# Edge scores of a graph attention layer with the leaky relu split, one decoding of the edge counts, and shorter lags between gathers, exponentials and scatters

## The chip, the cores and the metric

The kernel runs on one core of a Trainium2 chip, in one launch. The metric is device time in microseconds (us); the figure of the kernel before is the median of five runs. A profile is one further execution, recorded by the hardware profiler, and has a time of its own. Engines are named as the profile names them: PE is the matrix engine (PEld its weight loads), DVE the vector engine, ACT the scalar engine, POOL the GpSimd engine, SP the engine that issues most of the plain DMAs.

## The reference

A two-layer graph network on 625 nodes with 1024 features and 10,000 edges, sorted by their destination. Each layer adds to x the output of a graph layer and of a linear attention, both on the normalised x, and then that of a feed-forward block. Layer 0 has the graph attention that the change is about; layer 1 has two mean-aggregating layers, a linear attention, and a full attention with a mixture of experts. The graph attention, cut to what matters (h is 4 heads, d is 64):

```python
xl = (x @ Wl).reshape(n, H, D)          # 625 x 4 x 64
xr = (x @ Wr).reshape(n, H, D)
msg = xl[src] + xr[dst]                 # one row for each edge, and for each node with itself
act = jnp.where(msg > 0, msg, 0.2 * msg)
e = jnp.einsum('ehd,hd->eh', act, att)
p = jnp.exp(e - segment_max(e, dst)[dst])
alpha = p / (segment_sum(p, dst)[dst] + 1e-16)
out = segment_sum(alpha[..., None] * xl[src], dst)
```

An edge between the same two nodes may occur several times.

## The kernel before

Nodes lie in five tiles of 125 rows (t = 0 to 4). The whole computation is the function `attempt`, which is called with `shifted=False`; it leaves out the maximum in the softmax. Tests on the size of what occurred are collected in the columns of `inside`; if one fails, a second `attempt(shifted=True)` runs after the first (`again`), and computes the safe form.

Since a softmax weight depends only on the pair (source, destination), the kernel makes two dense tables. `CT` counts how often each pair occurs, and `table` in DRAM holds exp(score) for each pair. Then `weigh` (product in L743) multiplies a tile of the table, read back by `load_table` as `tb`, with the counts, which gives `pT`, and PE sums `pT` against xl1 (`pg`). xl1 holds the xl rows of each node, 64 for each head, and a 65th column for the denominator.

The counts are made on PE. For each of 79 columns of 128 edges (`EN`), DVE writes two one-hot rows into `ring` (L414, L416; up to 8 columns ahead), and PE adds five products to the PSUM tile `pct` (L437). To hold two destinations in one number, a count of the upper half of the destinations is weighted with 4096. `decode` (L448 to L456) takes the two apart on DVE. It runs three times, after columns 27, 53 and 79 (`counting`), and after each the counting pauses for two steps (`held`).

The scores are made on DVE for 40 groups, each of two columns of edges (the last has one column of 16 edges). The group's rows are gathered by POOL with four indirect DMAs, two into `ga` from xl and two into `gb` from xr (L578; four buffers of each kind). `score_group` adds them (L586) and calls `score` (L555): leaky relu (L557), product with `att` (L558), sum over each head's 64 (L559), and a clip at 60 (L561). ACT takes the exponential (L565), and POOL writes the group's results to `table` with two indirect DMAs (L592). The same for a node with itself is done by `self_loops` (L601), five times, on rows that lie in SBUF; there L607 also copies the xl rows into xl1.

The order on each engine is the order in which the program emits the work. `do` delays a stream's parts, so that preparation, PE work and what follows it are interleaved. `work(us)` (L613) is a clock by estimate: callers report PE time, and after each 7.6 us one beat g is emitted, in this order: a self loop (g = 1 to 5), the exponential of group g-4, the score of group g-3, then in turn the gathers of group g and the scatters of group g-5. So with 40 groups there are 45 beats. POOL and DVE work through these in order; each waits where its data or a buffer is not ready. The 79 column counts lie among the keys and values of the linear attention (two halves of five tiles, with up to six counts after each tile), and after them come its queries and answers (m = 0 to 7; `oT`), with the first products of the output projection (`mixed`, L668, `px`). Beats that are then left are emitted at once (L691), then `load_table(0)`, the sums of the weights of the feed-forward block (`weight_sums`, L707), their mean on PE (`pm`), the rest of `mixed`, and `weigh(0)`.

Later, in layer 1, the degrees of the nodes come out of another count (`pdeg`), with a test on the largest one (L1031, L1032), and the tests in `inside` are summed by a product on PE (`prt`).

Of the kernel before, what the change touches and what calls it, by code (L numbers as in the profile page):

```python
# [8 lines left out]
FP = mybir.dt.float32  # L9
# [4 lines left out]
AF = mybir.ActivationFunctionType  # L14
ALU = mybir.AluOpType
# [18 lines left out]
NB_MIN = 10  # L34
FAR = -1.0e30
LIMIT = 60.0
LEAST, MOST = 1.0e-22, 1.0e25
MAGIC = 12582912.0
BIG = 1.5 * 2.0**35

# [12 lines left out]
def attempt(ctx: ExitStack, tc: tile.TileContext, w: dict, out: bass.AP, shifted: bool):  # L53
# [26 lines left out]
    nc.vector.memset(blockmask[0:64, 0:64], 1.0)  # L80
    nc.vector.memset(blockmask[64:128, 64:128], 1.0)

    inside = const.tile([128, 3], FP, name="inside")
    nc.vector.memset(inside, 1.0)

    def test(col, src, n, pool):
# [251 lines left out]
    with ExitStack() as st0:  # L338
# [8 lines left out]
        with ExitStack() as edges:  # L347
# [51 lines left out]

            pad(xnT)  # L400
            nc.vector.memset(xl1[:, :, :, 64:65], 1.0)

            counting = [(lo, hi, t) for lo, hi in ((0, 27), (27, 53), (53, EN)) for t in range(lo, hi)]
            part = dict(done=0, held=0)
            made_ahead = []

# [10 lines left out]
            def count():  # L419

                if part["held"] or part["done"] == EN:
                    return False
                lo, hi, t = counting[part["done"]]
                part["held"] = 2 * (t == hi - 1)

                def prep():
                    while len(made_ahead) < min(8, EN - t):
                        one_hot()
                    hold["hot"] = made_ahead.pop(0)
                    part["done"] += 1  # L430

                def pe():
                    od, os = hold["hot"]
                    if t == lo:
                        part["pc"] = psums[-1][0].tile([128, NT, 512], FP, tag="pct", name="pct", bufs=1)
                    for j in range(NT):
                        nc.tensor.matmul(part["pc"][:P, j, :HN], lhsT=os[:, nodes(j)],  # L437
                                         rhs=od[:, :HN], start=(t == lo), stop=(t == hi - 1))

                def decode():  # L440
                    for j in range(0, NT, 2):
                        js = slice(j, min(j + 2, NT))
                        n = js.stop - j
                        low, high, v = CT[:, js, 0:HN], CT[:, js, HN:NP], part["pc"][:P, js, :HN]
                        low_r, high_r = CTr[:, js, 0:HN], CTr[:, js, HN:NP]
                        u = pool.tile([P, 2, HN], FP, tag="u", name="u", bufs=1)[:, 0:n, :]

                        nc.vector.tensor_scalar(u, v, 1728.0, BIG, op0=ALU.subtract, op1=ALU.add)  # L448
                        nc.vector.tensor_scalar(u, u, BIG, None, op0=ALU.subtract)
                        if lo == 0:  # L450
# [12 lines left out]
                do(prep, pe, decode if t == hi - 1 else None)  # L463
                return True
# [87 lines left out]

            def score(dst, m, n, p):  # L555

                nc.vector.scalar_tensor_tensor(m, m, 0.2, m, op0=ALU.mult, op1=ALU.max)  # L557
                nc.vector.tensor_tensor(m, m, att[0:p].unsqueeze(1).to_broadcast([p, n, 256]), op=ALU.mult)  # L558
                nc.vector.tensor_reduce(dst, m.rearrange("p t (h e) -> p t h e", h=4), AX.X, ALU.add)  # L559
                if not shifted:  # L560
                    nc.vector.tensor_scalar(dst, dst, LIMIT, None, op0=ALU.min)  # L561
# [20 lines left out]
            def score_group(g):  # L582
                lo, n, p = groups[g]
                a, b = ab.pop(g)
                m = a[0:p, 0:n, :]
                nc.vector.tensor_tensor(m, m, b[0:p, 0:n, :], op=ALU.add)  # L586
                score(es[0:p, lo:lo + n, :], m, n, p)

            def scatter(g, j):
                lo, n, p = groups[g]  # L590
                if j < n:
                    nc.gpsimd.indirect_dma_start(  # L592
                        out=table[:, :],
                        out_offset=bass.IndirectOffsetOnAxis(ap=at[0:p, lo + j:lo + j + 1], axis=0),
                        in_=es[0:p, lo + j, :], in_offset=None)

            own = pool.tile([P, NT, 4], FP, name="own")

            diagonal = table[0:N * (N + 1), :].rearrange("(s d) h -> s d h", d=N + 1)[:, 0, :]

            def self_loops(t):  # L601

                m = pool.tile([P, 1, 256], FP, tag="xd", name="gs", bufs=1)
                nc.vector.tensor_tensor(m[:, 0, :], xlr[:, t, 0:256], xlr[:, t, 256:512], op=ALU.add)
                score(own[:, t:t + 1, :], m, 1, P)
                exp(own[:, t:t + 1, :])
                nc.vector.tensor_copy(xl1[:, t, :, 0:64], xlr[:, t, 0:256].rearrange("p (h e) -> p h e", h=4))  # L607
                rows_dma(nc.scalar, diagonal[nodes(t), :], own[:, t, :])


# [1 line left out]

            def work(us):  # L613
                beat["us"] += us
                while beat["us"] >= 7.6 * beat["g"] and beat["g"] < len(groups) + 5:
                    g = beat["g"]
                    beat["g"] += 1
                    if 1 <= g <= NT:
                        self_loops(g - 1)
                    if 4 <= g < len(groups) + 4:  # L620
                        lo, n, p = groups[g - 4]
                        exp(es[0:p, lo:lo + n, :])
                    if 3 <= g < len(groups) + 3:
                        score_group(g - 3)
                    for j in range(G):
                        if g < len(groups):
                            gather(g, j)
                        if g >= 5:
                            scatter(g - 5, j)

            work(0.0)
            states = []
# [55 lines left out]
            nc.sync.dma_start(out=wu, in_=w["W_up"].rearrange("(k p) n -> p k n", p=128))  # L688
            bo = [lin.bias(w["L0_bo"], c, tag) for c, tag in enumerate(("bk_t", "bv_t"))]
            do.flush()  # L690
            while beat["g"] < len(groups) + 5:  # L691
                work(8.0)

        xpool = ctx.enter_context(tc.tile_pool(name="xpool", bufs=1, side="right", reuse_waits="tile"))
        x = xpool.tile([P, NT, D], FP, name="x")
# [322 lines left out]
    def degrees():  # L1018
        for t in range(NT):
            nc.vector.tensor_tensor(CTr[:, t, nodes(t)], CT[:, t, nodes(t)], ident[:P, :P], op=ALU.subtract)  # L1020

        def pe():
            pdeg = hold["pdeg"] = ps2("pdeg")
            for h in range(2):
                group(pdeg[:, h, :HN], [(ones[:P, :], CT[:, s, h * HN:(h + 1) * HN]) for s in range(NT)])

        def after():
            nc.vector.tensor_scalar(halves(dinv), hold["pdeg"][:, :, :HN], 1.0, None, op0=ALU.max)
            if not shifted:
                most = sage.tile([128, 1], FP, name="most")  # L1030
                nc.vector.tensor_reduce(most, dinv, AX.X, ALU.max)  # L1031
                nc.vector.tensor_scalar(inside[:, 1:2], most, 4095.0, None, op0=ALU.is_le)  # L1032

        do(None, pe, after)

# [622 lines left out]
    nc.vector.tensor_reduce(within, hold["prt"][:P, 2 * NT * NE:2 * NT * NE + 3], AX.X, ALU.add)  # L1658
    nc.vector.tensor_scalar(meta[:, NB + 1:NB + 2], within, -1.0, 384.0, op0=ALU.mult, op1=ALU.add)
# [74 lines left out]
    rest(NB_MIN)  # L1734
    again = None
    if not shifted:
        again = nc.values_load(meta[0:1, NB + 1:NB + 2], min_val=0, max_val=384,
                               skip_runtime_bounds_check_because="384 less three sums of up to 128 ones and zeros")


    with tc.manual_schedule(engines={mybir.EngineType.PE, mybir.EngineType.DVE, mybir.EngineType.Pool}):
# [121 lines left out]
```

## Time and profile before

| what | us |
|---|---|
| median of five runs | 2275.61 |
| the five runs | 2266.3 to 2280.53 |
| the profiled execution | 2269.82 |
| its span | 2268.0 |
| its mean granted PE clock | 0.969 of full speed |

What the profile says of the groups that the change touches:

| group | count | busy us | mean ns |
|---|---|---|---|
| L592 POOL, indirect scatter to `table` | 79 | 85.3 | 1080 |
| L578 POOL, indirect gather to `ga` | 79 | 81.7 | 1034 |
| L578 POOL, indirect gather to `gb` | 79 | 80.9 | 1024 |
| L437 PE, edge counts | 395 | 69.6 | 325 |

The graph attention lies between about 55 and 465 us of the span; POOL's first gather starts at 55.6 us, its last scatter at 446.0 us. A page gives busy times of each engine, the same over forty slices, and the chain of work that ended last; the trace behind it gives single instructions with what each waited for. An idle time is written as "[1.89 <-DMA table<-es,at]": the engine stood for 1.89 us before this instruction, and what came last was a DMA into `table`. "issue" there means that nothing which the profile shows was waited for.

### The profile page before, as it was taken

To read this page: it belongs to the slowest core of one execution; us is meant where nothing else is said; L and a number is where in the kernel's file an instruction comes from. 1 tells how busy PE (TensorE), PEld (TensorE's weight loads), DVE (VectorE), ACT (ScalarE), POOL (GpSimd) and SP (SyncE) were. 2 spreads that over 40 slices of the span, in tenths; PEclk is the share of its full clock that TensorE was granted. 3 is DMA by queue.
4 is the path that set the end of the run, shared out by engine and by line. 5 is a ranking of instruction groups with operands and counts; after the bars stand their busy time and mean duration, and the time that the engine had idled before them with its cause. 6 is when DMAs were issued, how large, how long until landed. Compare 5 with 4: busy or idle time off the path is not lost. (4 is left out here: it accounts for less than half of the span.)

```text
span 2268.0 us, 17398 instructions
## 1 busy us (share of the span) xinstructions
PE 2140.9 (94%) x6934; PEld 1217.3 (54%) x6934; DVE 754.1 (33%) x1265; ACT 193.4 (9%) x349; POOL 346.6 (15%) x351
## 2 busy tenths in 40 slices
PE   8879788898899989999999999999999999999998
PEld 6545446455444658764445776556754444444443
DVE  5758458956522373000112133332111111111112
ACT  2000001001110110000000011110000000000000
POOL 1566666510000040001000000010000000000010
PEclk9979799999999999999999999999999999999999
DMA  9324224152020220213211111030279997898742
GB/s 298 100 80 150 59 94 148 60 134 94 19 102 1 78 89 1 74 55 122 74 37 58 63 56 38 10 111 0 93 283 330 328 330 287 320 332 309 260 148 94
DMA packets 145849, 301.63 MB, mean 133 GB/s; under 512 B 12370, under 2 KB 22436, under 8 KB 145754
## 3 DMA queue, kind: packets, MB, share of 16 engines
q1 hardware_dynamic: 123412, 243.18, 30.0%
q0 software_dynamic: 17664, 47.47, 7.0%
q10 hardware_dynamic: 4678, 9.72, 1.4%
q8 instruction: 58, 0.95, 0.2%
q14 instruction: 37, 0.30, 0.0%
HBM read 277.49 MB, written 22.84 MB: 132 GB/s over the span
## 5 line engine op out<-in xcount | busy, mean ns | idle before, releaser
L129 PE MATMUL pu<-w,xgT 128*128 128x512 f32 x768 | 333.9, 593 | 1.9 <-DVE xgT L1157 1.9
L129 PEld LDWEIGHTS pu<-w,xgT 128*128 128x128 f32 x768 | 144.0, 190 | 174.8 <-issue 172.0
L129 PE MATMUL pyb<-w,hb 128*128 128x512 f32 x384 | 174.3, 598 | 2.4 <-ACT yb L104 2.1
L129 PE MATMUL pk<-w,xnT 128*125 128x512 f32 x320 | 149.3, 614 | 18.0 <-issue 12.0
L129 PE MATMUL pq<-xnT,w 128*128 128x313 f32 x512 | 144.1, 442 | 9.7 <-ACT qf L314 6.0
L129 PE MATMUL pv<-w,xnT 128*125 128x512 f32 x320 | 141.1, 593 | 1.4 <-ACT xnT L925 1.2
L129 PE MATMUL p<-tT,w 128*128 128x313 f32 x512 | 136.3, 428 | 0.4 <-DVE tT L1157 0.4
L129 PEld LDWEIGHTS pq<-xnT,w 128*128 128x128 f32 x512 | 99.8, 197 | 53.7 <-ACT qf L314 9.4
L1697 DVE TENSOR_TENSOR su<-pu,su 128x512 f32<-128x512 f32 x24 | 16.6, 692 | 314.6 <-ACT su L1696 314.6
L129 PEld LDWEIGHTS pyb<-w,hb 128*128 128x128 f32 x384 | 69.8, 189 | 90.9 <-issue 74.8
L129 PEld LDWEIGHTS p<-tT,w 128*128 128x128 f32 x512 | 96.8, 190 | 37.9 <-issue 1.2
L129 PEld LDWEIGHTS pk<-w,xnT 128*125 128x125 f32 x320 | 61.3, 194 | 98.2 <-issue 91.3
L129 PEld LDWEIGHTS pv<-w,xnT 128*125 128x125 f32 x320 | 59.6, 188 | 73.4 <-issue 71.7
L592 POOL DMA_INDIRECT table<-es,at x79 | 85.3, 1080 | 59.1 <-issue 31.7
L437 PE MATMUL pct<-ring 128*125 128x313 bf16 x395 | 69.6, 325 | 24.5 <-issue 23.5
L578 POOL DMA_INDIRECT ga<-xl_d,si x79 | 81.7, 1034 | 68.6 <-DVE es L559 27.9
L1680 POOL DMA_INDIRECT xg<-rows_d,slots x12 | 11.4, 947 | 524.8 <-PE pxg L1687 449.0
L578 POOL DMA_INDIRECT gb<-xr_d,di x79 | 80.9, 1024 | 24.1 <-issue 24.1
L437 PEld LDWEIGHTS <-ring 128*125 128x125 bf16 x395 | 57.4, 149 | 42.0 <-issue 40.3
L668 PE MATMUL px<-w,oT 128*125 128x512 f32 x160 | 74.6, 622 | 5.6 <-DVE oT L333 4.0
L1047 DVE TENSOR_TENSOR z<-pz,z 125x512 fp32r<-125x512 f32 x10 | 6.9, 692 | 196.8 <-ACT z L1045 196.8
L129 PE MATMUL px<-w,hT 128*125 128x512 f32 x160 | 70.3, 592 | 0.0
(359 smaller groups left out, 2596.6 us busy)
## 6 DMA issues: line engine op xcount, KB each, us to landing
w<-in_eW_dram SPq DMA_DIRECT2D x144, 1024.0 KB
w<-in_L_Wk_dram SPq DMA_DIRECT2D x8, 1024.0 KB
w<-in_L_Wv_dram SPq DMA_DIRECT2D x8, 1024.0 KB
w<-in_L_Wq_dram SPq DMA_DIRECT2D x8, 1024.0 KB
w<-in_L_Wo_dram SPq DMA_DIRECT2D x8, 1024.0 KB
w<-in_W_self_dram SPq DMA_DIRECT2D x8, 1024.0 KB
w<-in_W_neigh_dram SPq DMA_DIRECT2D x8, 1024.0 KB
w<-in_sW_dram SPq DMA_DIRECT2D x8, 1024.0 KB
```

Source lines behind the costliest of these rows:

```text
L129: nc.tensor.matmul(dst, lhsT=lhsT, rhs=rhs, start=(i == 0), stop=(i == len(pairs) - 1))
L437: nc.tensor.matmul(part["pc"][:P, j, :HN], lhsT=os[:, nodes(j)], rhs=od[:, :HN], start=(t == lo), stop=(t == hi - 1))
L578: nc.gpsimd.indirect_dma_start(out=dst[0:p, j, :], out_offset=None, in_=src[:, :], in_offset=bass.IndirectOffsetOnAxis(ap=ix[0:p, lo + j:l ...
L592: nc.gpsimd.indirect_dma_start(out=table[:, :], out_offset=bass.IndirectOffsetOnAxis(ap=at[0:p, lo + j:lo + j + 1], axis=0), in_=es[0:p, l ...
L668: nc.tensor.matmul(hold["px", t][:P, c, :], lhsT=oT[:, k, nodes(t)], rhs=wo[c](k), start=(k == 0), stop=False)
L1047: nc.vector.tensor_tensor(low, src, high.bitcast(FP), op=ALU.subtract)
L1680: nc.gpsimd.indirect_dma_start(out=xg, out_offset=None, in_=rows_d[:, :], in_offset=bass.IndirectOffsetOnAxis(ap=slots[:, b:b + 1], axis=0))
L1697: nc.vector.tensor_tensor(su, pu[:, 0, :], su, op=ALU.mult)
```

## The change

A leaky relu with slope 0.2 is 0.2 m + 0.8 max(m, 0). So a score is a linear part, the sum of 0.2 att (xl[src] + xr[dst]), and the sum of 0.8 att max(m, 0). In the linear part, the share of the destination is the same for all edges of a destination and cancels in the softmax; the share of the source is a factor exp(0.2 att xl) for each node and head. The change computes only the relu part for edges, with `att` multiplied by 0.8 once, and puts the factor of the source into xl1: the 64 rows of a head are multiplied with it, and the 65th column, which was 1, holds it. `self_loops` computes that factor for its tile (product, sum, clip, exponential on ACT, product), in place of the copy. The clip's limits are tested in a fourth column of `inside` (`test_linear`).

The counts are decoded once, after all 79 columns, with another offset for rounding; the test of the degrees becomes tighter and also compares their sum with the number of edges. The lags of `work` become 3 for the exponential, 2 for the score and 3 for the scatter, and there are 43 beats instead of 45. The order within a beat stays.

```diff
+            if not shifted:
+                nc.vector.tensor_scalar(att, att, 0.8, None, op0=ALU.mult)
...
-            counting = [(lo, hi, t) for lo, hi in ((0, 27), (27, 53), (53, EN)) for t in range(lo, hi)]
+            counting = [(lo, hi, t) for lo, hi in (((0, 27), (27, 53), (53, EN)) if shifted else ((0, EN),))
+                        for t in range(lo, hi)]
...
-                        nc.vector.tensor_scalar(u, v, 1728.0, BIG, op0=ALU.subtract, op1=ALU.add)
+                        nc.vector.tensor_scalar(u, v, 1728.0 if shifted else 2047.0, BIG, op0=ALU.subtract, op1=ALU.add)
...
             def score(dst, m, n, p):
 
-                nc.vector.scalar_tensor_tensor(m, m, 0.2, m, op0=ALU.mult, op1=ALU.max)
-                nc.vector.tensor_tensor(m, m, att[0:p].unsqueeze(1).to_broadcast([p, n, 256]), op=ALU.mult)
+                by_att = att[0:p].unsqueeze(1).to_broadcast([p, n, 256])
+                if shifted:
+                    nc.vector.scalar_tensor_tensor(m, m, 0.2, m, op0=ALU.mult, op1=ALU.max)
+                    nc.vector.tensor_tensor(m, m, by_att, op=ALU.mult)
+                else:
+                    nc.vector.scalar_tensor_tensor(m, m, 0.0, by_att, op0=ALU.max, op1=ALU.mult)
                 nc.vector.tensor_reduce(dst, m.rearrange("p t (h e) -> p t h e", h=4), AX.X, ALU.add)
...
+            def test_linear():
+                c = pool.tile([P, NT, 4], FP, name="clipped")
+                nc.vector.tensor_scalar(c, linear, -4.0 * LINEAR, 4.0 * LINEAR, op0=ALU.max, op1=ALU.min)
+                nc.vector.tensor_tensor(c, c, linear, op=ALU.is_equal)
+                nc.vector.tensor_reduce(inside[:P, 3:4], c, AX.XY, ALU.min)
...
-                nc.vector.tensor_copy(xl1[:, t, :, 0:64], xlr[:, t, 0:256].rearrange("p (h e) -> p h e", h=4))
+                rows = xlr[:, t, 0:256].rearrange("p (h e) -> p h e", h=4)
+                if shifted:
+                    nc.vector.tensor_copy(xl1[:, t, :, 0:64], rows)
+                else:
+                    nc.vector.tensor_tensor(m[:, 0, :], xlr[:, t, 0:256], att[:P], op=ALU.mult)
+                    nc.vector.tensor_reduce(linear[:, t, :], m.rearrange("p t (h e) -> p (t h) e", h=4), AX.X, ALU.add)
+                    part4 = pool.tile([P, 4, 1], FP, tag="part4", name="part4", bufs=2)
+                    nc.vector.tensor_scalar(part4[:, :, 0], linear[:, t, :], -4.0 * LINEAR, 4.0 * LINEAR,
+                                            op0=ALU.max, op1=ALU.min)
+                    nc.scalar.activation(xl1[:, t, :, 64:65], part4, AF.Exp, scale=0.25)
+                    nc.vector.tensor_tensor(xl1[:, t, :, 0:64], rows,
+                                            xl1[:, t, :, 64:65].to_broadcast([P, 4, 64]), op=ALU.mult)
                 rows_dma(nc.scalar, diagonal[nodes(t), :], own[:, t, :])
...
-                while beat["us"] >= 7.6 * beat["g"] and beat["g"] < len(groups) + 5:
+                while beat["us"] >= 7.6 * beat["g"] and beat["g"] < len(groups) + 3:
...
-                    if 4 <= g < len(groups) + 4:
-                        lo, n, p = groups[g - 4]
+                    if g >= 3:
+                        lo, n, p = groups[g - 3]
                         exp(es[0:p, lo:lo + n, :])
-                    if 3 <= g < len(groups) + 3:
-                        score_group(g - 3)
+                    if 2 <= g < len(groups) + 2:
+                        score_group(g - 2)
                     for j in range(G):
                         if g < len(groups):
                             gather(g, j)
-                        if g >= 5:
-                            scatter(g - 5, j)
+                        if g >= 3:
+                            scatter(g - 3, j)
...
-            while beat["g"] < len(groups) + 5:
+            while beat["g"] < len(groups) + 3:
                 work(8.0)
+            if not shifted:
+                test_linear()
...
-                nc.vector.tensor_scalar(inside[:, 1:2], most, 4095.0, None, op0=ALU.is_le)
+                nc.vector.tensor_scalar(inside[:, 1:2], most, 4094.0, None, op0=ALU.is_le)
+
+                nc.vector.tensor_reduce(most, hold["pdeg"][:, :, :HN], AX.XY, ALU.add)
+                nc.vector.tensor_scalar(most, most, float(E), None, op0=ALU.is_equal)
+                nc.vector.tensor_tensor(inside[:, 1:2], inside[:, 1:2], most, op=ALU.mult)
...
-        group(hold["prt"][:P, 2 * NT * NE:2 * NT * NE + 3], [(ones[:, :P], inside)])
+        group(hold["prt"][:P, 2 * NT * NE:2 * NT * NE + 4], [(ones[:, :P], inside)])
```

`inside` is one column wider (four of 128 ones, so 512 where 384 stood), and the upper limit of another test, `MOST`, goes from 1e25 to 1e16.

More of the change, by code (lines that the diff above doesn't have):

```diff
@@ L36 @@
 LIMIT = 60.0
-LEAST, MOST = 1.0e-22, 1.0e25
+LINEAR = 20.0
+LEAST, MOST = 1.0e-22, 1.0e16
 MAGIC = 12582912.0
@@ L81, in attempt @@
     nc.vector.memset(blockmask[64:128, 64:128], 1.0)
-    inside = const.tile([128, 3], FP, name="inside")
+    inside = const.tile([128, 4], FP, name="inside")
     nc.vector.memset(inside, 1.0)
@@ L597, in attempt @@
             own = pool.tile([P, NT, 4], FP, name="own")
+            linear = pool.tile([P, NT, 4], FP, name="linear")
+            def test_linear():
[3 more added lines that the diff above has]
+                nc.vector.tensor_reduce(inside[:P, 3:4], c, AX.XY, ALU.min)
             diagonal = table[0:N * (N + 1), :].rearrange("(s d) h -> s d h", d=N + 1)[:, 0, :]
@@ L1657, in attempt @@
     within = pool.tile([P, 1], FP, name="within")
-    nc.vector.tensor_reduce(within, hold["prt"][:P, 2 * NT * NE:2 * NT * NE + 3], AX.X, ALU.add)
-    nc.vector.tensor_scalar(meta[:, NB + 1:NB + 2], within, -1.0, 384.0, op0=ALU.mult, op1=ALU.add)
+    nc.vector.tensor_reduce(within, hold["prt"][:P, 2 * NT * NE:2 * NT * NE + 4], AX.X, ALU.add)
+    nc.vector.tensor_scalar(meta[:, NB + 1:NB + 2], within, -1.0, 512.0, op0=ALU.mult, op1=ALU.add)
     nc.vector.tensor_scalar(meta[:, 0:NB], exp_f, float(NE - 1), None, op0=ALU.min)
@@ L1736, in attempt @@
     if not shifted:
-        again = nc.values_load(meta[0:1, NB + 1:NB + 2], min_val=0, max_val=384,
-                               skip_runtime_bounds_check_because="384 less three sums of up to 128 ones and zeros")
+        again = nc.values_load(meta[0:1, NB + 1:NB + 2], min_val=0, max_val=512,
+                               skip_runtime_bounds_check_because="512 less four sums of up to 128 ones and zeros")
     with tc.manual_schedule(engines={mybir.EngineType.PE, mybir.EngineType.DVE, mybir.EngineType.Pool}):
```

## The prediction

> **What bounds the kernel now.** I read five views in this order: busy times and slices of the page, busy time by stretch, the waits of POOL, the timeline of single instructions, and the chain that ended last. Slices first (one is 56.7 us); the change lies in slices 2 to 9.
>
> ```profile
> PE 2140.9 (94%) x6934; PEld 1217.3 (54%) x6934; DVE 754.1 (33%) x1265; ACT 193.4 (9%) x349; POOL 346.6 (15%) x351
> PE   8879788898899989999999999999999999999998
> DVE  5758458956522373000112133332111111111112
> POOL 1566666510000040001000000010000000000010
> PEclk9979799999999999999999999999999999999999
> PE 3%; DVE 0%; issue 0%
> ```
>
> PE is 94% busy and the chain is nearly all PE: a gain must be time in which PE stands or runs slowly. Such time lies where POOL works (slices 2 to 8). By stretch (columns: stretch, length, PE, PEld, DVE, ACT, POOL busy, clock, DMA share, GB/s):
>
> ```profile
> 74.00:88.00 14.00, 7.19 (x27) 4.99 (x25) 3.19 (x8) 1.26 (x2) 5.41 (x6) 0.65 0.23 67
> 100.00:131.00 31.00, 31.00 (x105) 16.87 (x104) 28.71 (x63) 3.13 (x8) 24.27 (x23) 1.00 0.21 61
> 131.00:160.00 29.00, 14.29 (x37) 6.58 (x36) 7.87 (x22) 0.21 (x1) 17.29 (x18) 0.59 0.19 55
> 220.00:258.00 38.00, 21.48 (x48) 9.76 (x47) 11.67 (x27) 0.42 (x2) 23.95 (x25) 0.61 0.20 57
> 300.00:351.00 51.00, 34.62 (x121) 23.76 (x120) 18.29 (x31) 5.88 (x15) 33.88 (x33) 0.80 0.47 160
> 351.00:428.00 77.00, 75.21 (x266) 49.87 (x266) 73.10 (x79) 10.91 (x23) 51.15 (x48) 1.00 0.31 97
> 428.00:442.00 14.00, 6.01 (x11) 2.28 (x11) 13.26 (x11) 0.20 (x1) 4.79 (x5) 0.80 0.01 1
> ```
>
> Full stretches (PE 31 of 31, clock 1.00) alternate with four poor ones, where PE is empty for 6.8, 14.7, 16.5 and 16.4 us (54.4) and runs at reduced clock besides. Holding every matmul start against the best interval of its kind, I get 10.9, 22.8, 27.6 and 25.2 us lost, 86 us in all. The single instructions say how it begins and ends (start, length, engine, line, what it waited for):
>
> ```profile
> 137.77 0.42 PE L437 MATMUL pct<-ring 128*125 128x313 bf16 x1 [0.91 <-issue]
> ...
> 250.02 1.00 POOL L592 DMA_INDIRECT table<-es,at  x1 [0.30 <-issue]
> 257.90 1.03 POOL L578 DMA_INDIRECT ga<-xl_d,si  x1 [6.88 <-DVE es L559]
> ```
>
> In a poor stretch PE's instructions come one by one with waits on nothing named, DVE stands too, and POOL goes on issuing indirect DMAs. A stretch ends soon after POOL stops at a gather whose buffer DVE has not freed: POOL stands 251.0 to 257.9, PE is full again from 258; 153.5 to 163.4, and PE full from 160. Why a POOL stream slows PE this trace does not say; one run of POOL (257.9 to 290.2) has no poor stretch, so it is not a rule without exception. POOL's own waits between 55 and 415, then its end:
>
> ```profile
> POOL ga L578 <- DVE es L559: 27.9, 3, 11.0
> POOL ga L578 <- DVE es L561: 12.9, 8, 5.7
> 440.30 0.96 POOL L592 DMA_INDIRECT table<-es,at  x1 [1.89 <-DMA table<-es,at]
> 446.01 1.79 POOL L592 DMA_INDIRECT table<-es,at  x1 [1.91 <-DMA table<-es,at]
> ```
>
> After the last gather (414.0) 11 scatters go alone, 2.74 us apart (418.65 to 446.01), each behind an earlier DMA; then tb is loaded, DVE weighs it (457.9 to 462.8), and PE takes it at 465.0 without a wait, since px covers: about 2.2 us of slack.
>
> **The change, part by part.** The sum goes against the profiled 2269.8 us (span 2268.0); that is 5.8 under the median 2275.6, so 5.8 is added at the end.
>
> Score. L557 and L558 become one operation. Starts of one group at 111.81 and 112.53 give 0.72 a step; 39 x 0.72 = 28 us of DVE in 57 to 430. Where DVE stands in the poor stretches this is worth nothing. In 351:428 DVE is busy 73.1 of 77 and PE 75.2, both at their limit; 10 groups there give DVE 7 us, but PE has only 1.8 us empty. Taken: -2, ends 0 and -3.
>
> Decoding once. The first decode took 6.7 us (113.33 to 120.04); those at 195.39 and about 280 some 10.6 and 10. One of 6.7 remains, so 20 us of DVE go and two pauses of the count. PE is full around all three: 0, ends 0 and -3 (the one PE wait on v, 3.4 us). The cover is PE's keys and values, with one-hot rows made up to 8 ahead.
>
> Self loops, five. Removed: L558 0.46 and the copy 0.20 (starts 70.27 to 70.47). Added: two passes over 256 columns (0.45 each, as L558 and L559), a clip (0.17), an ACT exponential and a product (0.45) that waits for it. DVE +0.9 and a handover; the nearest row is kf behind ACT kb, which waited 0.79 for a longer ACT step. Queued behind that product are the next group's score and v, behind them POOL's gather. 5 x (0.9 to 1.7) = 4.5 to 8.5 us of DVE between 65 and 100, where PE is fed by rows made ahead: +1, ends 0 and +8. The test of three small operations, the scaling of att and the degree test (its reduce like L1031's 805 ns, and no one waits): +1 together, ends 0 and +2.
>
> Lags. Per beat POOL issues 4 gathers and 2 scatters; their number stays 158 and 79, so 237 x 1.28 = 303 us of issue stay (durations 1.02 to 1.08 and 0.30 between). Each score moves a beat ahead of the gathers, the exponentials too, the scatters two. This does two things. It moves 4 scatters (2 beats x 2) from the end to the front: before, 22 gather calls on POOL precede the first scatter, afterwards 14. And it shortens how far POOL runs ahead. Before, with DVE at beat p POOL may finish beat p+1; afterwards its scatter needs the exponential of the same beat, so it stops after the first pair of p+1: 4 DMAs earlier, 4 x 1.28 = 5.1 us. So when PE and DVE slow down, POOL stops 5.1 us sooner, and if its stop is what frees them, each poor stretch is 5.1 us shorter. At the start the new wait falls at the first scatter, about 73.6, just before the first poor stretch (74:88, 10.9 lost). Taken: -8 of these 10.9, ends 0 and -10.9. For the three others 3 x 5.1 = 15; as POOL then also stops more often, with PE's L437 stream untouched, I take -10, ends 0 and -75.6 (all of their loss) on one side. On the other, if POOL's stops are mere lost time to it, +20 (below). DVE returns sooner to the group that POOL waits for, 2 groups x 0.72 per stop: -3, ends 0 and -4.
>
> What is late next is POOL. PE's work in 57:428 is 371 less 86 = 285 us, under POOL's 303. POOL cannot end before 55.6 + 303 + 5 x 1.4 = 366, against 447.8: no more than 82 us can be had here.
>
> End. Six scatters or fewer go alone instead of 11: 5 x 2.7 = 13 us earlier, on top of what POOL gains earlier. This must give way when PE comes sooner (its slack is 2.2); it does: beats left over are emitted before L707's sums, and there are two fewer. The last group's score leaves DVE before the answer that px waits for (PE empty 4.0 at 429, 4.0 at 437.6): -3, ends 0 and -8.
>
> Sum: -2 +1 +1 -8 -10 -3 -3 = -24: 2245.8 by the profile, 2252 by the median; taken 2250.
>
> Two rules of the skill beside rows. Row: gb at 69.91 takes 0.95 us while the copy runs (70.27 to 70.56), as do its neighbours without one, so taking five copies away gives POOL nothing. The Trainium skill, page "SBUF — State Buffer", section "A bandwidth-pool intuition that's wrong (but worth ruling out)", says that such a DMA beside a DVE tensor_copy takes about 3.1 us for 0.62; by it the five copies would be worth 5 x 2.5 = 12 us to POOL, against this row. Row: lone scatters follow each other by 2.74 us. The page "DMA: Bandwidth & Descriptors", section "Anatomy of one DMA — SWDGE (gpsimd) path", fits about 2.0 us to each; by it the shorter end would save 5 x 2.0 = 10 instead of 13, an estimate from that page.
>
> **The rivals.**
>
> A, slower: POOL becomes the longest chain. The place is the scatter of each beat, which now waits for an exponential that DVE and ACT have only just been able to make. For it: POOL's 303 exceed PE's 285, and a stop costs it 5.1 us at each poor stretch (20 for four). Handing from DVE to ACT to POOL, at about 0.8 a beat (the kf wait), adds up to 40 x 0.8 = 32 where nothing lies between. Against it: the end gets 13 shorter, and POOL already waits 41 us for es. It decides once POOL loses over 2 + 13 + 3 = 18 us net of shorter poor stretches; at 20 + 16 (half the beats) - 18 it gives +18: 2294.
>
> B, nothing on the path: the poor stretches have their own cause and length, and DVE's 48 us fall in covered time. For it: the run 257.9 to 290.2 without a stretch, and the one at 300 which begins while POOL has just started again. Only the query stage and the end gain: -2 -3 = -5: 2270.
>
> C, the poor stretches go: they begin 19, 31, 27 and 39 us after POOL starts to issue without a stop. If stops of each beat keep its runs below 19 us, most of 86 goes, up to POOL's limit of 82: -70, 2205. Against it: POOL has more work than PE, and stops only once DVE is late.
>
> D: the tests fail and the second attempt runs, roughly doubling the time. The clipped and the counted values pass with room for inputs of this size; under 1 in 100.
>
> **How the numbers follow.** Chances: main 0.52 (-12 to -45, so 2230 to 2264), C 0.15, B 0.17, A 0.16. 0.5% is 11.4 us, about what a measurement here can tell from none (the five runs spread 14). Main and C are faster, 0.67; B the same, 0.17; A slower, 0.16. The range takes in half of C and the lower half of A: 2207 to 2288, with some 0.16 left out.
>
> **What would show it.** Right: the first pause of POOL at about 74 waits on ACT; 74:88 runs at clock near 1.00; three poor stretches remain, each near 5 us shorter; five or six scatters follow the last gather; pg takes its operand without a wait; DVE busy is about 42 us less (754 to 712). Wrong: poor stretches as long as before (B), POOL waiting on ACT es in most beats and PE waiting for pT or oT (A), or PE full through 57:350 (C). A poor stretch at a new place would show that the trigger is not POOL's run length at all.

## The result and the profile after

The change makes no difference that counts: 2281.64 us median (52 runs) against 2277.66 us for the kernel before (94 runs), a ratio of 1.0012 (0.12% slower) with a 95% interval of 1.0002 to 1.0023. The profiled execution has a span of 2281.3 us against 2268.0 us, which is 13 us more; the runs of each kernel spread over 29 us and more, so this one pair says little about size. It says more about where the time goes.

The page of the changed kernel, busy times, slices and chain:

```profile
PE 2140.1 (94%) x6934; PEld 1215.8 (53%) x6934; DVE 712.0 (31%) x1212; ACT 194.2 (9%) x354; POOL 344.8 (15%) x351
PE   7959769898889998999999999999999999999998
DVE  4836336767442274000013132432111111111112
POOL 1665566520000022001000000020000000000010
PEclk9979889899899999999999999999999999999999
PE 3%; DVE 0%; issue 0%
```

DVE has 42 us less to do (754.1 to 712.0), so the work did go. PE's work is the same, and so is the low share of PE in slices 2 to 8. By stretch (columns as before):

```profile
74.00:88.00 14.00, 14.00 (x57) 8.43 (x56) 12.14 (x32) 2.50 (x8) 8.96 (x9) 1.00 0.23 65
127.00:172.00 45.00, 19.68 (x45) 8.35 (x45) 12.31 (x32) 0.42 (x2) 27.97 (x28) 0.62 0.21 59
228.00:274.00 46.00, 33.06 (x66) 11.84 (x65) 11.13 (x19) 1.56 (x4) 29.16 (x30) 0.85 0.20 58
300.00:340.00 40.00, 19.71 (x80) 15.19 (x79) 11.48 (x21) 3.50 (x12) 26.60 (x26) 0.74 0.21 60
```

The first poor stretch (74:88) is gone, PE is full there at clock 1.00. The second has grown instead, from 29 to 45 us. By the same account as before (each matmul start against the best interval of its kind) PE now loses 95 us up to 423, where it lost 89 up to 428 (86 of them in the four stretches). The three stretches that are left lose 34.9, 22.1 and 25.3 us, 82 in all, where they lost 75.6.

What DVE waited for in 55:450 (engine, line, cause: total us, times, longest). The kernel before has no wait of DVE on a gather's DMA in its list:

```profile
DVE ga L596 <- DMA gb<-xr_d,di: 51.9, 14, 7.4
DVE v L269 <- remote: 40.7, 2, 26.6
DVE ga L596 <- issue: 10.5, 3, 5.7
```

So DVE comes to a score sooner, and stands until POOL has gathered its rows. POOL in turn still waits for scores in this profile, now at its scatters, three times and up to 16.2 us long; the kernel before had waited 46.9 us for es:

```profile
POOL table L602 <- ACT es L575: 36.6, 3, 16.2
```

POOL's last instructions of the stage (start, length, cause of the idle time before):

```profile
424.00 1.27 POOL L588 DMA_INDIRECT gb<-xr_d,di  x1 [0.30 <-issue]
425.57 1.02 POOL L602 DMA_INDIRECT table<-es,at  x1 [0.30 <-issue]
428.00 0.97 POOL L602 DMA_INDIRECT table<-es,at  x1 [1.40 <-DMA table<-es,at]
...
445.66 0.85 POOL L602 DMA_INDIRECT table<-es,at  x1 [1.90 <-issue]
```

Seven scatters follow the last gather instead of eleven. But the last gather itself is at 424.0 where it was at 414.0, so the last scatter (445.7) is where it was (446.0). POOL began 3.3 us later (58.9), and up to the last gather its waits on its own earlier scatters grew from 5.7 to 19.7 us, more than its waits for es fell.

### The profile page after: what moved, and what is told of

The parts are those of the page before. It is cut to its first block, busy times and chain, and to the rows that moved or that the text cites. A ratio compares the mean times of both kernels' runs of the same rounds, so it can differ in the third digit from the quotient of the medians.

```text
span 2281.3 us, 17353 instructions
## 1 busy us (share of the span) xinstructions
PE 2140.1 (94%) x6934; PEld 1215.8 (53%) x6934; DVE 712.0 (31%) x1212; ACT 194.2 (9%) x354; POOL 344.8 (15%) x351
## 5 line engine op out<-in xcount | busy, mean ns | idle before, releaser
L130 PE MATMUL pu<-w,xgT 128*128 128x512 f32 x768 | 333.9, 593 | 1.9 <-DVE xgT L1192 1.9
L130 PEld LDWEIGHTS pu<-w,xgT 128*128 128x128 f32 x768 | 144.0, 190 | 174.8 <-issue 172.0
L130 PE MATMUL pyb<-w,hb 128*128 128x512 f32 x384 | 174.3, 598 | 2.4 <-ACT yb L105 2.1
L130 PE MATMUL pv<-w,xnT 128*125 128x512 f32 x320 | 146.6, 601 | 12.4 <-issue 10.4
L130 PE MATMUL pk<-w,xnT 128*125 128x512 f32 x320 | 145.3, 605 | 6.2 <-DVE x L940 4.7
L130 PE MATMUL pq<-xnT,w 128*128 128x313 f32 x512 | 142.6, 438 | 7.3 <-DVE v L269 6.1
L130 PE MATMUL p<-tT,w 128*128 128x313 f32 x512 | 136.3, 428 | 0.4 <-DVE tT L1192 0.4
L130 PEld LDWEIGHTS pq<-xnT,w 128*128 128x128 f32 x512 | 99.5, 196 | 49.8 <-DVE v L269 6.9
L130 PEld LDWEIGHTS pyb<-w,hb 128*128 128x128 f32 x384 | 69.8, 189 | 90.9 <-issue 74.8
L130 PEld LDWEIGHTS p<-tT,w 128*128 128x128 f32 x512 | 96.8, 190 | 37.9 <-issue 1.2
L130 PEld LDWEIGHTS pv<-w,xnT 128*125 128x125 f32 x320 | 59.7, 189 | 89.7 <-issue 86.6
L130 PEld LDWEIGHTS pk<-w,xnT 128*125 128x125 f32 x320 | 60.4, 192 | 84.1 <-issue 77.1
L602 POOL DMA_INDIRECT table<-es,at x79 | 82.7, 1047 | 94.8 <-ACT es L575 36.6
L441 PE MATMUL pct<-ring 128*125 128x313 bf16 x395 | 63.3, 307 | 26.1 <-issue 26.0
L588 POOL DMA_INDIRECT ga<-xl_d,si x79 | 80.4, 1018 | 31.8 <-issue 22.7
L697 PE MATMUL px<-w,oT 128*125 128x512 f32 x160 | 76.0, 632 | 7.1 <-DVE oT L334 4.0
L130 PE MATMUL px<-w,hT 128*125 128x512 f32 x160 | 70.3, 592 | 0.0
L130 PE MATMUL px<-w,oT 128*125 128x512 f32 x160 | 70.3, 592 | 0.0
```

The costliest lines, as they stand in the source:

```text
L130: nc.tensor.matmul(dst, lhsT=lhsT, rhs=rhs, start=(i == 0), stop=(i == len(pairs) - 1))
L588: nc.gpsimd.indirect_dma_start(out=dst[0:p, j, :], out_offset=None, in_=src[:, :], in_offset=bass.IndirectOffsetOnAxis(ap=ix[0:p, lo + j:l ...
L602: nc.gpsimd.indirect_dma_start(out=table[:, :], out_offset=bass.IndirectOffsetOnAxis(ap=at[0:p, lo + j:lo + j + 1], axis=0), in_=es[0:p, l ...
L697: nc.tensor.matmul(hold["px", t][:P, c, :], lhsT=oT[:, k, nodes(t)], rhs=wo[c](k), start=(k == 0), stop=False)
```

## The experiments

All runs below stand beside runs of the kernel before on the same chip (four chips in all). There that kernel takes 2242 to 2244 us, 34 us less than the 2277.66 above; of the figures above the chip isn't known. So the profiles of the two kernels were taken again (before_again, after_again). Ratios are to the kernel before on the same chip. "Last gather", "pT" and "pg" are the starts of POOL's last gather, of DVE's first product with the table and of PE's first sum with it; "px" is the start of the 24 products of tile 0 with the output projection, which follow the last query; "wait" is what DVE waited for DMAs of gathers in 55:450.

| run | ratio (95%) | DVE busy | wait | px | last gather | pT | pg |
|---|---|---|---|---|---|---|---|
| before_again | 1.0001 (0.999 to 1.0012) | 754.8 | 52.7 | 375.1 | 385.3 | 426.9 | 428.1 |
| decode_only | 0.9988 (0.9977 to 0.9998) | 734.4 | 72.0 | 379.8 | 390.0 | 431.7 | 432.8 |
| score_only | 0.9995 (0.9986 to 1.0005) | 732.7 | 67.5 | 375.1 | 385.7 | 427.4 | 428.5 |
| old_lags | 0.9998 (0.9984 to 1.0011) | 713.0 | 84.3 | 370.0 | 380.8 | 423.2 | 424.3 |
| lags_only | 0.9999 (0.9988 to 1.0009) | 754.8 | 66.2 | 390.9 | 389.3 | 428.2 | 438.6 |
| after_again | 0.9986 (0.9974 to 0.9997) | 712.6 | 104.0 | 390.8 | 389.9 | 427.6 | 438.1 |

### The parts of the change, one by one

lags_only is the kernel before with this edit:

```diff
-                while beat["us"] >= 7.6 * beat["g"] and beat["g"] < len(groups) + 5:
+                while beat["us"] >= 7.6 * beat["g"] and beat["g"] < len(groups) + 3:
...
-                    if 4 <= g < len(groups) + 4:
-                        lo, n, p = groups[g - 4]
+                    if g >= 3:
+                        lo, n, p = groups[g - 3]
...
-                    if 3 <= g < len(groups) + 3:
-                        score_group(g - 3)
+                    if 2 <= g < len(groups) + 2:
+                        score_group(g - 2)
...
-                        if g >= 5:
-                            scatter(g - 5, j)
+                        if g >= 3:
+                            scatter(g - 3, j)
```

> The kernel before with the three new lags and nothing else. Theory R (run-ahead: PE creeps while POOL streams, until POOL stops; shorter lags make POOL stop earlier, as the prediction had it): 2277.7 - 8 (start) - 10 (three later stretches) - 3 (end) = about 2257, ratio 0.991. Theory P (the shorter lags shorten no stretch in sum, because a stretch that POOL leaves sooner is followed by a sooner or longer one): ratio 0.998 to 1.004, poor stretches in sum 80 to 100 us as before (86). Theory W (the new wait on the exponential costs what the rest of the change saves): ratio 1.005 or more, and POOL's waits on es grow by over 10 us.

decode_only is the kernel before with one range of counts:

```diff
-            counting = [(lo, hi, t) for lo, hi in ((0, 27), (27, 53), (53, EN)) for t in range(lo, hi)]
+            counting = [(lo, hi, t) for lo, hi in ((0, EN),) for t in range(lo, hi)]
...
-                        nc.vector.tensor_scalar(u, v, 1728.0, BIG, op0=ALU.subtract, op1=ALU.add)
+                        nc.vector.tensor_scalar(u, v, 2047.0, BIG, op0=ALU.subtract, op1=ALU.add)
```

> The kernel before with the counts decoded once and nothing else. Theories R and P: the 20 us of DVE that go lay beside full PE, ratio 0.998 to 1.002. Theory W: 0.993 to 0.997. DVE busy about 734 us in all of them.

old_lags is the changed kernel with the first diff above undone; score_only is that with the second diff's ranges and offset put back as well.

> The changed kernel with the three old lags, so score split and one decoding together. Theory R: the gain of the lags is missing, so slower than the changed kernel by some 15 us if that gain is there: but the changed kernel measured 1.001, so R needs here a ratio of about 1.007 to 1.010. Theory P: 0.997 to 1.002, no different from the changed kernel beyond the interval. Theory W: clearly faster than the changed kernel, 0.985 to 0.993, since the 43 us of DVE are saved and the wait on the exponential is not added.

> The changed kernel with the old lags and with the counts decoded in three ranges: what is left is the split score with its self loops and tests. Theory R: DVE stands anyway in the poor stretches, so only the query stage gains: ratio 0.997 to 1.000. Theory P: 0.998 to 1.002. Theory W: the split saves 28 us of DVE and some of it reaches PE, so that the lags can eat it: 0.990 to 0.995. In all three DVE is busy about 754 - 28 + 5 = 731 us.

All four ratios lie within 0.12% of 1, in the ranges of theory P. The lags alone did not shorten the stage (theory R), nor do they eat a gain of the rest (theory W): without them nothing is gained either. The column "wait" says why. One decoding takes 20.4 us of DVE work away and adds 19.3 us of waiting for gathers; the split score takes 22.1 away and adds 14.8; both together 41.8 and 31.6. What DVE does not do, it mostly waits. The waits of DVE in before_again and in after_again:

```profile
DVE ga L586 <- DMA gb<-xr_d,di: 52.7, 14, 8.1
```

```profile
DVE ga L596 <- DMA gb<-xr_d,di: 104.0, 25, 8.4
```

### Is it POOL's stream that sets the pace?

> The kernel before, unchanged, for its profile and time on the same chip as the three runs with it. Ratio 1.000 +- 0.002. Theory Q (POOL's stream of 237 indirect DMAs is the chain that sets the end of the stage, whatever DVE saves): nearly no waits of POOL on es, and PE waiting for pT or with lost time enough to hide it. Theory D (DVE and PE set the pace and POOL waits for them): POOL waits on es for over 30 us, as in the profile of before that the prediction used.

> The changed kernel, unchanged. Both theories: ratio 0.999 to 1.003, as measured. Theory Q: the last gather is issued within 10 us of that of the kernel before on the same chip, though 43 us of DVE work are gone. Theory D: the last gather at another time by over 10 us, and the difference is seen in POOL's waits on es.

In before_again POOL waits less than 9 us for es in all; it issues nearly without a stop from 56.0 on, and its last gather comes 4.6 us before that of the changed kernel, though that has 42 us less DVE work. Its largest waits are on its own earlier DMAs (view of the waits, POOL, 50:450):

```profile
POOL table L592 <- DMA table<-es,at: 33.0, 17, 3.7
...
POOL table L592 <- ACT es L565: 6.9, 2, 5.3
```

From the first gather to the last (56.0 to 385.3) lie 39 beats and 329 us, so 8.4 us a beat, where `work` reckons 7.6.

Three runs change the work of one engine. no_count leaves out nearly all of the products of the edge counts:

```diff
-                    for j in range(NT):
+                    for j in range(NT if t in (lo, hi - 1) else 0):
                         nc.tensor.matmul(part["pc"][:P, j, :HN], lhsT=os[:, nodes(j)],
```

> The changed kernel without the products of the edge counts, but for the first and last column (385 of 395 matmuls of L441 left out, some 60 us of PE work; the counts and so the output are wrong, DVE's one-hot rows are still made). Theory Q: POOL's stream is as long as before, so the last gather is issued at most 15 us earlier and the whole gains 0 to 20 us. Theory D: PE's work comes to its end 50 to 60 us sooner, the time falls by 45 us or more.

The kernel's tests saw the missing counts and started the second attempt, so the whole time (6521.61 us) compares with nothing; the stage in question lies in the first attempt and can be read. Busy times by stretch up to the last gather, of no_count and then of after_again:

```profile
57.00:385.00 328.00, 241.53 (x690) 133.47 (x689) 203.24 (x401) 32.12 (x87) 238.00 (x230) 0.86 0.36 114
```

```profile
57.00:390.00 333.00, 287.98 (x1072) 182.52 (x1071) 204.88 (x406) 32.82 (x90) 238.90 (x231) 0.92 0.37 114
```

PE is busy for 46 us less, and the stage is 5 us shorter: last gather at 385.2 (389.9), pg at 433.3 (438.1). PE waits for DVE instead, and DVE for gathers (100.7 us).

pool_extra adds a memset on POOL (of a tile of its own) after each gather call, and no DMA:

```diff
                             gather(g, j)
+                            nc.gpsimd.memset(extra, 0.0)
```

> The changed kernel with one POOL memset of 128 x 512 floats after each of the 80 gather calls, so POOL gets longer by 80 times some 0.5 us (the trace will say), with no DMA added. Theory Q: the time grows by 0.7 to 1.0 of what is added, 25 to 45 us. Theory D: POOL has slack (its waits on es were 37 us in the changed kernel), the time grows by less than 10 us.

```profile
L658 POOL MEMSET extra<- 128x512 f32 x80 | 44.4, 555 | 0.0
```

The time is 2268.07 us, ratio 1.0108 (1.0082 to 1.0133), 27.7 us over after_again: 0.62 of the 44.4 us that were added, a little under theory Q's 0.7. POOL's waits on earlier scatters fell from 25.4 to 18.8 us, and its pauses before scatters with no named cause from 22.7 to 14.2, so a part of the memsets filled time in which POOL stood. The edit isn't quite of POOL alone: the 39 clips of the scores on DVE (L571) took 520 ns each in place of 172, and DVE was busy for 726.6 us in place of 712.6. But DVE waited longer for gathers than without the memsets (117.8 us against 104.0), and POOL waited 2.8 us for es, so DVE had not become the slower of the two. The last gather is 27.8 us later (417.7), as much as the whole is longer, to a tenth.

no_scatter takes the other side, POOL's work away:

```diff
-                if j < n:
+                if j < n and shifted:
                     nc.gpsimd.indirect_dma_start(
                         out=table[:, :],
```

> The changed kernel without the 79 scatters (the table keeps its fill, so the softmax sees only self loops and the output is wrong; all DVE and ACT work stays). Theory Q (POOL's stream sets the pace; DVE waits for gathers and PE for DVE): POOL has 158 gathers, 158 x 1.28 = 202 us instead of about 330, so DVE's wait for gathers (104 us in the changed kernel on the chip of the runs before) falls below 30 us, the last gather comes at 300 or earlier unless the beats, emitted by PE time, hold it back to about 350, and the time falls by 40 to 70 us against the kernel before. Theory D: the stage stays as long, only the lone scatters at the end go, 0 to -12 us.

DVE's wait for gathers falls to 1.9 us, now POOL waits for DVE, and pg starts at 377.3, 61 us before that of after_again. PE is then busy for 371.6 of the 383 us in 57:440, against 331.4 in after_again: this is what the stage costs when PE sets the pace.

```profile
POOL ga L588 <- DVE es L571: 46.1, 14, 11.8
```

The whole gained only 0.67% (0.9933, 0.9916 to 0.995), 15 us, where 40 to 70 had been expected. With other values the routing of the last block chose one expert block more: 832 products L130 pu where the others have 768, and 416 pyb for 384, and from pg to the end it is 45 us longer (1847.5 against 1802.3). That comes of the values, which differ without the scatters; the 61 us of the stage lie ahead of it.

Theory Q holds in all of these, on the chips of these runs: POOL's stream is the chain, DVE waits for it, and PE for DVE.

### What the shorter lags do

They have two effects, and px and pg show both. PE's products and the table's end in before_again and then in after_again (timeline of PE):

```profile
375.11 10.56 PE L668 MATMUL px<-w,oT 128*125 128x512 f32 x24 [0.25 <-ACT qf L314]
...
405.16 23.07 PE L668 MATMUL px<-w,oT 128*125 128x512 f32 x48
428.07 0.35 PE L129 MATMUL pg<-xl,pT 125*125 125x65 f32 x2
428.94 0.43 PE L129 MATMUL pg<-xl,pT 125*125 125x65 f32 x2 [0.52 <-DVE pT L743]
```

```profile
390.81 10.56 PE L697 MATMUL px<-w,oT 128*125 128x512 f32 x24
...
415.70 22.54 PE L697 MATMUL px<-w,oT 128*125 128x512 f32 x48
438.08 2.19 PE L130 MATMUL pg<-xl,pT 125*125 125x65 f32 x19
```

With the old lags px starts 10.2 us ahead of POOL's last gather (10.2 to 10.8 in the four runs that have them), then PE has its products done and waits for pT, tile by tile, because eleven scatters and the table's load come first. With the new lags px starts 0.9 us after the last gather (lags_only: 1.6), whatever DVE has to do, so PE's own work is what pg waits for. A score that DVE has one beat sooner in its order asks one beat sooner for its gathers. Where POOL sets the pace, this holds back everything behind it on DVE, here 11 to 12 us relative to the last gather, and PE with it. That uses up what the shorter end of POOL's stream gains. On the sums of the second tile the two kernels are 3.7 us apart (458.4 and 462.2), less than at pg, since PE no longer waits tile by tile.

If this is so, the gain must appear once DVE's order is given time. A beat of 9.0 us instead of 7.6 does that with one number:

```diff
-                while beat["us"] >= 7.6 * beat["g"] and beat["g"] < len(groups) + 3:
+                while beat["us"] >= 9.0 * beat["g"] and beat["g"] < len(groups) + 3:
```

beat_84 has 8.4 there; before_beat_90 is the kernel before with 9.0, b90_old_lags and b90_lags_only are old_lags and lags_only with it.

> The changed kernel with a beat of 9.0 instead of 7.6 us of estimated PE work, so DVE meets each group's gathers about when POOL, at 330 us for 40 beats, can have made them. Theory Q: DVE's wait for gathers inside the queries and keys falls from 104 to under 50 us, PE ends the queries 20 to 40 us sooner, POOL's last gather stays at about 390, and pg starts at 420 to 425 instead of 438: the time falls by 10 to 18 us (ratio 0.992 to 0.995 to the kernel before). Theory D: the longer beat only delays the gathers: ratio 1.005 or more.

> The changed kernel with a beat of 8.4 us. Theory Q: about half of the gain of 9.0, ratio 0.994 to 0.997. Theory D: ratio 1.002 or more.

> The kernel before with a beat of 9.0 us and nothing else. Theory Q: the queries end sooner here too, but 11 scatters still go alone after the last gather (30 us, against 21 with the short lags), so pT waits for the table: a gain of 0 to 8 us, and at least 6 us slower than the changed kernel with this beat, which would be what the change is worth once POOL's pace is met. Theory D: ratio 1.005 or more.

> The changed kernel with the old lags and a beat of 9.0 us: score split and one decoding, without the shorter lags. Theory L (of the 0.8% between the two kernels at this beat nearly all is the shorter end of POOL's stream, since DVE has time to spare): ratio 1.000 to 1.003, like the kernel before at this beat (1.0019), with 10 or 11 scatters alone and pT waiting for the table. Theory S (the saved DVE work carries it): ratio 0.993 to 0.996.

> The kernel before with the new lags and a beat of 9.0 us, score and decoding as before. Theory L: ratio 0.992 to 0.996, like the changed kernel at this beat (0.9938). Theory S: 0.999 to 1.003.

| run | ratio (95%) | wait | last gather | last scatter | pT | pg |
|---|---|---|---|---|---|---|
| before_beat_90 | 1.0019 (1.0009 to 1.0028) | 25.2 | 393.2 | 424.7 | 435.4 | 436.5 |
| b90_old_lags | 0.9989 (0.9974 to 1.0005) | 23.0 | 384.8 | 416.4 | 427.3 | 428.4 |
| b90_lags_only | 0.9961 (0.9947 to 0.9975) | 47.0 | 394.2 | 413.6 | 425.7 | 428.6 |
| beat_84 | 0.9940 (0.9923 to 0.9957) | 84.8 | 390.9 | 410.5 | 422.4 | 424.9 |
| beat_90 | 0.9938 (0.9917 to 0.9960) | 74.6 | 390.5 | 409.2 | 421.1 | 425.9 |

The changed kernel gains 0.6% at both beats, the kernel before loses 0.2%: at this beat the change is worth 0.8%, 16 us between two medians (2230.58 and 2246.81 us). Of it the lags alone bring 0.6% and the DVE work alone 0.3% (these two on another chip, so by their ratios), so theory L is right for the larger part, and S is not nothing. Neither ratio lies in a range that was expected: 0.9961 is just outside L's, and 0.9989 between those of L and S. The kernel before was expected to gain 0 to 8 us at this beat and lost 4. The expectation for beat_84 (half the gain) was wrong: it has all of it, with 0.9940 on the edge of the range. In beat_90 PE now stands elsewhere:

```profile
PE pm L130 <- DVE part L738: 35.3, 1, 35.3
```

PE has ended its queries (px starts at 343.9 instead of 390.8) and waits for three sums that DVE does behind the last scores. early_sums is beat_90 with these sums emitted ahead of the beats that are left over:

```diff
+            part3 = const.tile([128, 3], FP, name="part3")
+            for i in range(3):
+                nc.vector.tensor_reduce(part3[:, i:i + 1], raw[i], AX.X, ALU.add, apply_absolute_value=True)
             while beat["g"] < len(groups) + 3:
                 work(8.0)
...
-        part3 = late.tile([128, 3], FP, name="part3")
...
-        weight_sums()
```

> The changed kernel with a beat of 9.0 us, and the three sums of weights (L738, 6.7 us of DVE) emitted ahead of the beats that are left over. At this beat PE waited 35.3 us for them, as they stood behind the last scores, which wait for POOL. Theory Q: PE's wait for part is gone, px runs while POOL ends its stream, pT starts when tb has come (about 414), pg at 415 to 420 instead of 426: 6 to 12 us less than the same kernel without it, ratio 0.988 to 0.992. Otherwise (PE bound after all): ratio 0.993 to 0.995.

```profile
PE pg L130 <- DVE pT L776: 37.8, 5, 36.8
```

```profile
410.05 0.85 POOL L602 DMA_INDIRECT table<-es,at  x1 [1.90 <-issue]
412.66 0.89 POOL L164 DMA_DIRECT2D tb<-table  x1 [1.76 <-DMA table<-es,at]
```

The wait moved, whole, to the table: pT at 420.7 (421.1), pg at 421.8, ratio 0.9964 (0.9951 to 0.9977), no better than beat_90's (on another chip). The expectation of 0.988 to 0.992 was wrong because it took pT as possible at 414; the table's load is only issued at 412.7 and pT starts 8 us behind it. PE is idle for 37 us there. As long as the table ends no sooner, less work on PE or DVE has nothing further to gain at this place.

## Why the prediction was wrong

**Where it failed.** The step is the price of the lags: "if its stop is what frees them, each poor stretch is 5.1 us shorter", with -8 and -10 of the sum of -24. It took PE for the bound and POOL's pauses for the end of the poor stretches. In the profile after, which has the whole change, the first stretch went (-10.9 where -8 was taken), but the three others lost 82 us where 75.6 less 10 had been forecast: POOL still stopped up to 16.2 us long. On the chips of the experiments POOL hardly pauses, PE waits for DVE and DVE for gathers, and the lags alone give 0.9999.

**The mis-sized term.** The prediction named the right successor ("what is late next is POOL") and sized it too small: 303 us of issue, done at 366 at the earliest. Measured with hardly any wait for DVE: 56.0 to 417.1 in before_again, 361 us. Of the difference, 33 us are waits on its own earlier DMAs, of which the prediction counted 7; some 18 are the issue itself, since the 237 DMAs last 1.05 us on average, with 0.30 between (the prediction's own durations, 1.02 to 1.08, give more than its 1.28); the last 7 are mostly waits for es. The profile that the prediction read had the row: the stream's 247.9 us of busy time, 76 us of pauses with no named cause and 21 us of waits on its own DMAs are 345 us without any wait for DVE or ACT. With 345 us in place of 303 the room above POOL is 47 us instead of 82, and it is made of POOL's waits for es: only what shortens these can bring POOL's end forward. On the chips of the experiments they are 8 us in before_again, so a saving on PE or DVE had next to no room there.

**DVE's part.** Priced at 0 to -3 for each edit: right, but not for the reason that was named, that PE is full around it. The 42 us came out as forecast (712 us, measured 712.0), and on the chips of the experiments they turned into waiting for gathers.

**The end of POOL's stream.** "5 x 2.7 = 13 us earlier" is somewhat high: from the last gather to the last scatter it is 30.0 us in before_again and 21.1 in after_again, 9 us less. By the prediction's own count four scatters move to the front, so seven are left and not "six or fewer". The "-3" for the last score's earlier place is wrong in sign where POOL sets the pace: the lag that brings it forward holds the queries back by 11 to 12 us.

**The start.** 74:88 did run at clock 1.00, as forecast; but the next stretch lost 12.1 us more (22.8 to 34.9).

**The rivals.** B's time (2270) lies nearest to the result. Its reason, that the stretches have a cause of their own, stays untested, as the experiments ran where PE's one-by-one instructions don't occur; there DVE's saved work was no covered time but turned into waiting. A named the mechanism, POOL as the longest chain, and gave it +18 us; on the chips of the experiments it was the longest already before, so making DVE quicker changed nothing. Its sign, POOL waiting on ACT for es in most beats, did not appear (three waits in the profile after). C did not occur.

**The rule beside the row.** score_only, where the five copies are gone, has its last gather at 385.7 against 385.3, so the row's 0 stands. The 12 us were an estimate from the 3.1 us in the Trainium skill, page "SBUF — State Buffer", section "A bandwidth-pool intuition that's wrong (but worth ruling out)". The same section says that such a DMA is blocked until the end of the DVE operation and about 115 ns more; for a copy of 0.29 us that is far less than 2.5, so the estimate did not follow from it.

**What stays open.** In the profile that the prediction read, PE's instructions come one by one with no named cause; in the changed kernel's profile of the same setting they still do, and in after_again the same products run without a gap. First the changed kernel there, then after_again (timeline of PE):

```profile
133.20 0.29 PE L441 MATMUL pct<-ring 128*125 128x313 bf16 x1 [0.95 <-issue]
133.93 0.29 PE L441 MATMUL pct<-ring 128*125 128x313 bf16 x1 [0.43 <-issue]
135.33 0.29 PE L441 MATMUL pct<-ring 128*125 128x313 bf16 x1 [1.11 <-issue]
```

```profile
153.30 4.16 PE L441 MATMUL pct<-ring 128*125 128x313 bf16 x30
```

The same two settings are 34 us apart in the time of one and the same kernel. What causes it was not found, and whether the longer beat helps there was not tried. That POOL's stream holds the changed kernel back there too is argued from DVE's 52 us of waits for gathers, not shown: in the same profile POOL waits 36.6 us for es.

## What to carry to other kernels

Look for the engine that nobody waits for by name: in before_again PE was 95% busy and waited for DVE, and DVE for DMAs, while the engine that issues these DMAs, at 15% of the span, put out one after the other and set the pace of the stage. Before pricing a shorter lag, compare the interval at which the producer really delivers (8.4 us a beat) with the one that the order assumes (7.6): where the producer is slower, a shorter lag puts the wait in front of other work on the consumer's queue. When a saving turns up as waiting time elsewhere, give that engine's order more slack, and see whether the saving appears.

## What was not expected

The same kernel takes 2277.66 us in the one set of runs and 2242 to 2244 us on the chips of the experiments, with PE's instructions one by one in the one and not in the other. Other values (no_scatter) moved the time by one expert block, about 45 us, more than any part of the change did. And adding 44.4 us of memsets to the engine that sets the pace cost only 27.7 us; 15 of the other 17 are pauses of POOL that became shorter (6.6 and 8.5 us).
